# A DiT-style block of six attention layers and an FP4 feed-forward: the last layer's gate applied in its weights, FP4's margin in the scale, bias preparation moved off VectorE, stage priorities that change in time

## The chip, the cores and the metric

The kernel runs on one core of one Trainium2 chip. Times are device microseconds of one execution; a few executions are given as median with lowest and highest. The profile is of one more execution, and its span runs from the first to the last instruction of that execution.

The core's engines work side by side, each through its own queue in order: TensorE (PE: matmuls and transposes; PEld is its weight load), VectorE (DVE), ScalarE (ACT), GpSimd (POOL), and SyncE (SP), which here only issues DMAs. Results of TensorE land in PSUM, which has eight banks.

## The reference

Eight batches of 1024 tokens with 128 features, all float32. Cut to what matters:

```python
mod = (silu(c) @ wmod).reshape(8, 6, 1, 128)         # sa, ca, ga, sb, cb, gb
ga, gb = sign(ga) * max(|ga|, 0.25), likewise gb      # sign(0) = +1

h = layernorm(x) * (1 + ca) + sa
for i in range(6):                                    # 8 heads of 16
    xn = layernorm(h) * ln1_w[i] + ln1_b[i]
    q, k, v = softmax(xn @ wq[i], over 16), softmax(xn @ wk[i], over tokens), xn @ wv[i]
    h = (q @ (k.T @ v)) @ wo[i] + bo[i] + h           # per head
    xn = layernorm(h) * ln2_w[i] + ln2_b[i]
    h = leaky(xn @ w1[i]) @ w2[i] + h                 # 128 -> 512 -> 128
x = x + ga * h

h = layernorm(x) * (1 + cb) + sb
h = silu(fp4(h) @ fp4(w_gate).T) * (fp4(h) @ fp4(w_up).T)    # 128 -> 352
x = x + gb * (fp4(h) @ fp4(w_down).T)                        # 352 -> 128
```

`fp4` scales each block of 16 values by its largest magnitude over 6, rounds each to the grid 0, 0.5, 1, 1.5, 2, 3, 4, 6 (a value in the middle goes down), and scales back.

## The kernel before

A batch is one tile of 128 partitions by 1024 columns (8 chunks of 128 tokens), worked in two halves of 512 columns. Four batches are in flight at a time, each in a lane with its own buffers; batch 4 follows batch 0 in lane 0, and so on. All weights are loaded into SBUF once, within the first 50 us.

The program is not written in the order in which it runs. The function `tile_adaln_kernel` adds steps to a plan: an engine, an estimated duration, a function that issues the instructions, what it reads and writes. `Plan.order` (lines 142 to 206) then simulates the engines with these durations and picks, again and again, the step that can start earliest, and among those the one with the largest sum of its longest path to the end ("tail") and a lead. It also picks PSUM banks. It models GpSimd and some VectorE steps (`port=True`) as excluding each other. The order found is fixed for every engine's queue. Where TensorE would stand idle for longer than `GAP`, filler matmuls (`warm`, line 1250) are put in.

The leads are the table `LEAD`: for each of the eight batches eight numbers, one for each stage, where stage 0 is the first norm, 1 to 6 are the layers and 7 is the FFN. Steps added under `aside` (modulation, bias preparation) have a small negative lead of their own instead.

The parts that the change touches:

- `prepare_attn` (lines 500 to 540), once per layer: a matmul makes the 128 values that ln1's bias gives through wv; VectorE copies them out broadcast to 128x128 (line 512); a matmul with wo follows; VectorE adds bo (526) and divides by the number of heads (531); VectorE scales the rows of wv by ln1's weight (536).
- `fp4` (lines 640 to 712): largest magnitude of each block (658), over 6 with a floor (665), reciprocal (670), the reciprocal times minus one and a hair (675), the product (680), magnitude times 2^22 as bfloat16 on ScalarE (690), two VectorE steps that round by adding and subtracting a large number (694, 701), and the product with the scale on GpSimd (708). The hair, 2^-22, makes values in the middle go down.
- `prepare_ffn` (lines 715 to 766): the FP4 of the three weights, their transposes, and ScalarE's copies (749, 764).
- `layer` (from line 855): the MLP makes four hidden tiles per half (matmul 1063, ScalarE 1072), then 16 matmuls per half (1080), and VectorE adds the result onto the residual x (`onto_x`, line 1029).
- the main loop (from line 1203): after the six layers, VectorE multiplies each half of x by the gate ga (1228) and GpSimd adds the batch's input x0 (1236). Then comes `ffn`, whose `modulated_norm` takes the statistics of x (559).

Of the kernel before, what the change touches and what calls it, by code (L numbers as in the profile page):

```python
# [21 lines left out]
ROUND = 1.5 * UNIT  # L22
BANK = 512
# [59 lines left out]
class Plan:  # L83
# [7 lines left out]
    def __init__(self):  # L91
        self.steps, self.wrote, self.read, self.on = [], {}, {}, {}
        self.lead, self.batch = 0.0, -1

    def add(self, eng, occ, fn, r=(), w=(), func=None, port=False):

        s = Step()
        s.eng, s.occ, s.fn, s.func, s.lead = eng, occ, fn, func, self.lead  # L100
        s.batch, s.port = self.batch, port or eng == "POOL"
        s.lat, s.n, s.deps, s.outs = self.LAT[eng], len(self.steps), set(), []
        s.ps = list(dict.fromkeys(x for x in (*r, *w) if isinstance(x, Ps)))
        for x in s.ps:
            x.users += 1

        def keys(things):
            for x in things:
                if isinstance(x, Buf):
                    yield from x.parts  # L110
                else:
                    yield x

        r, w = list(keys(r)), list(keys(w))
        for x in (*r, *w):
            if isinstance(x, Part):
                tag = x.buf.tag
                if x.buf.after is None:
                    x.buf.after = self.on.get(tag, set())
                    self.on[tag] = set()  # L120
                s.deps |= x.buf.after
                self.on[tag].add(s.n)
        for x in (*r, *w):
            if x in self.wrote:
                s.deps.add(self.wrote[x])
        for x in w:
            s.deps.update(self.read.get(x, ()))
        for x in r:
            self.read.setdefault(x, []).append(s.n)
        for x in w:  # L130
            self.wrote[x], self.read[x] = s.n, []
        s.deps.discard(s.n)
        for x in s.ps:


            if x.first is None:
                x.first = s
            else:
                x.first.deps.update(d for d in s.deps if d < x.first.n)
        self.steps.append(s)  # L140

    def order(self, warm):
# [14 lines left out]
        table, port_free = None, 0.0  # L157
        out, todo = [], len(steps)
        while todo:
            banks = sorted(bank_free)  # L160
            best = None
            for e, c in cand.items():
                for n in c:
                    s = steps[n]
                    t = max(free[e], ready[n], port_free if s.port else 0.0)
                    need = sum(x.bank is None for x in s.ps)
                    if need:
                        t = max(t, banks[need - 1])
                    if t < INF:
                        cost = SWITCH if s.func and table and s.func != table else 0.0  # L170


                        pick = (t + cost, -s.tail - s.lead, n, t, cost)
                        if best is None or pick < best[1]:
                            best = (e, pick)
# [13 lines left out]
            end = t + cost + s.occ  # L189
# [52 lines left out]
def kernel(  # L242
# [41 lines left out]
        [1790.16, 1590.63, -133.39, -357.74, -170.79, -746.20, -949.01, -1084.50],  # L284
        [-328.73, -887.78, 125.60, 74.06, -1565.69, -372.37, -623.33, -863.15],
        [207.64, -149.66, -1586.32, -941.39, -1592.66, 94.98, -1452.11, -1239.07],
        [-746.08, 404.44, -824.95, -647.90, -118.96, -127.38, -1745.97, -425.45],
        [542.33, -1490.70, -1058.13, -1440.16, -391.61, -339.71, -149.19, -1160.38],
        [-1848.97, 2004.30, 268.43, 1104.45, -662.40, -326.99, -708.65, -1359.47],
        [573.17, -93.03, 284.47, -756.78, -278.27, -748.61, 318.91, -1786.29],  # L290
        [968.46, -558.77, 587.25, -611.65, -410.32, -941.76, -1400.05, -882.04],
    ]
    NQ = 4
# [12 lines left out]
    def stage(b, i):  # L306
        plan.lead, plan.batch = LEAD[b][i], b * len(LEAD[b]) + i

    @contextmanager
    def aside(late=40.0):  # L310

        kept = plan.lead, plan.batch
        plan.lead, plan.batch = -late, -2
        yield
        plan.lead, plan.batch = kept
# [22 lines left out]
    def load(dst, src, key, kb=64):  # L338

        if plan.batch == -1:  # L340
# [55 lines left out]
    plan.lead = 0.0  # L396
# [103 lines left out]
    def prepare_attn(l):  # L500
        t = Ps(psum)
        bv = Buf(work, [P, P], "bv", f"bv_{l}")
# [8 lines left out]
            "DVE", vec(P),  # L511
            lambda: nc.vector.tensor_copy(bv.ap(), t.ap()[:, :1].to_broadcast([P, P])),
# [5 lines left out]
                t.ap()[:, D : 2 * D], bv.ap(), wo_sb[:, l, :], start=True, stop=True  # L518
# [3 lines left out]

# [3 lines left out]
            lambda: nc.vector.tensor_tensor(mb, t.ap()[:, D : 2 * D], mb, ALU.add),  # L526
# [3 lines left out]
            "DVE", 0.14,  # L530
            lambda: nc.vector.tensor_scalar(mb, mb, 1.0 / HEADS, None, ALU.mult),
            w=[("mb", l)], port=True,
        )
        add(
            "DVE", 0.2,
            lambda: nc.vector.tensor_scalar(
                wv_sb[:, l, :], wv_sb[:, l, :], col(0, l), None, ALU.mult
            ),
            r=["cols"], w=[("wv", l)], port=True,
# [100 lines left out]
    def fp4(src, parts, ncol, n, i):  # L640

        nb = ncol // BLK
# [8 lines left out]
        def each(t):  # L651
# [13 lines left out]
            lambda: nc.vector.tensor_scalar(s(), s(), 1.0 / 6.0, 1e-12, ALU.mult, ALU.max),  # L665
# [5 lines left out]
        )  # L671

        add(
            "DVE", 0.08,
            lambda: nc.vector.tensor_scalar(r(), r(), 2.0**-22 - 1.0, None, ALU.mult),
            w=[rec], port=True,
# [18 lines left out]
                vv(), mm_(), ROUND, vv(), ALU.max, ALU.add  # L695
# [19 lines left out]
    def prepare_ffn():  # L715
# [20 lines left out]
        for n in range(2):  # L736
            t = Ps(psum)

            def turn(t=t, n=n):
# [9 lines left out]
                lambda t=t, n=n: nc.scalar.copy(wguT[:, n, :], t.ap()[:, :I]),  # L749
# [12 lines left out]
        def evict_d():  # L762
            for i, (k, kk) in enumerate(KS):
                nc.scalar.copy(wdT[:kk, i, :], u.ap()[:kk, i * D : (i + 1) * D])
# [90 lines left out]
    def layer(x, b, l, ln):  # L855
# [196 lines left out]
        _, xmT = normed(ln, x, "C", "A", l, 2, f"m{n}")  # L1052
        for h in range(H):
# [23 lines left out]
            def ymm(ty=ty, hidden=hidden):  # L1077
                for c in range(HC):
                    for j in range(NJ):
                        nc.tensor.matmul(  # L1080
                            ty.ap()[:, c * D : (c + 1) * D], hidden(j)[:, c * P : (c + 1) * P],
                            w2_sb[:, l, j, :], start=(j == 0), stop=(j == NJ - 1),
                        )

            add("PE", HC * NJ * mm(D), ymm, r=[*hT, ("w2", l)], w=[ty])
# [115 lines left out]
    for b in range(B):  # L1201
# [13 lines left out]
        for l in range(L):  # L1215
# [4 lines left out]
            layer(x, b, l, ln)  # L1220
# [3 lines left out]

        for h in range(H):
            add(
                "DVE", vec(HW),
                lambda x=x, mod=mod, h=h: nc.vector.tensor_tensor(
                    chunks(half(x, h)), chunks(half(x, h)),
                    over(mod.ap()[:, 2, :], HC), ALU.mult,  # L1230
                ),
                r=[mod[1]], w=at(x, h), port=True,
            )
            add(
                "POOL", pool2(HW) + 0.2,
                lambda x=x, b=b, h=h: nc.gpsimd.tensor_tensor(
                    half(x, h), half(x, h), half(x0s[b], h), ALU.add
                ),
                r=at(x0s[b], h), w=at(x, h),
            )  # L1240
# [18 lines left out]
    for step in plan.order(warm):  # L1259
# [50 lines left out]
```

## Time and profile before

| | |
|---|---|
| runs shown (3) | median 1429.36 us, 1426.54 to 1430.04 |
| profiled execution | 1430.2 us, its span 1428.5 us |
| TensorE clock granted | 0.999 |
| filler matmuls (line 1250) | 388 records, 49.8 us, the first at 1.6, the last at 1421.1 us |
| gate, line 1228 | 16 VectorE instructions, median 691 ns, 679 to 1466 |
| adding x0, line 1236 | 16 GpSimd instructions, median 1274 ns, 1264 to 1923 |
| matmuls of L1063 and L1080 | 350.4 and 468.3 us of TensorE's 1415.8 busy |
| stores of the result | 16 DMAs of 256 KB, 2.0 us from issue to landing |

A matmul in float32 shows as two records. Records of pipelined matmuls overlap a little, so their sum is somewhat above the time that they take in a row. The page also cuts the span into 40 equal slices, with the busy share of each engine in tenths:

```profile
PE   9999999999999999999999999999999999999998
PEld 7787877878787887877787788878887877886887
DVE  7896776667787985798978978987796775989986
ACT  5776777566677777676776867785677677777763
POOL 2020101001121220112112212111221001222232
```

TensorE is busy in every slice, but filler is among it. VectorE varies from 60% to over 90%, ScalarE is below 80% nearly everywhere, GpSimd is mostly idle. The DMA engines work in the first two slices, when the weights come in, and little afterwards.

### The profile page before, as it was taken

How to read it: one execution, taken by the hardware profiler on the slowest of the kernel's cores; microseconds unless marked ns; L12 is line 12 of the kernel's file. 1: busy time of each engine (PE TensorE's matmuls, PEld its weight loads, DVE VectorE, ACT ScalarE, POOL GpSimd, SP SyncE). 2: the span in 40 equal slices, each digit the busy share in tenths (PEclk: the TensorE clock that was granted, in tenths of full speed). 3: DMA queues.
4: the chain of work that ended last, by engine and by line, in shares of the span. 5: the costliest groups of instructions: out<-in, count | busy, mean ns of one | idle time of the engine just before them, and what ended most of it. 6: DMA issues, size and time to landing. Idle time of an engine off the chain costs nothing.

```text
span 1428.5 us, 26720 instructions
## 1 busy us (share of the span) xinstructions
PE 1415.8 (99%) x9395; PEld 1140.9 (80%) x9395; DVE 1146.0 (80%) x4560; ACT 995.9 (70%) x2280; POOL 241.8 (17%) x207
## 2 busy tenths in 40 slices
PE   9999999999999999999999999999999999999998
PEld 7787877878787887877787788878887877886887
DVE  7896776667787985798978978987796775989986
ACT  5776777566677777676776867785677677777763
POOL 2020101001121220112112212111221001222232
PEclk9999999999999999999999999999999999999999
DMA  7100000000000000000000000100000000000000
GB/s 214 47 1 1 1 1 1 1 1 1 1 22 6 16 1 1 1 27 16 1 1 28 8 1 8 27 1 8 9 1 1 1 1 1 1 16 1 16 16 15
DMA packets 16006, 18.81 MB, mean 13 GB/s; under 512 B 1552, under 2 KB 9848, under 8 KB 15872
## 3 DMA queue, kind: packets, MB, share of 16 engines
q1 hardware_dynamic: 15872, 17.10, 3.8%
q8 instruction: 74, 1.21, 0.3%
q14 instruction: 60, 0.49, 0.1%
HBM read 12.88 MB, written 4.22 MB: 12 GB/s over the span
## 4 chain that ended last, share of the span: by engine, by line
PE 82%; DVE 14%; ACT 2%; issue 1%; POOL 0%; DMA 0%; SPq 0%; DVEq 0%; POOLq 0%
PE ps L1080 23%; PE ps L1063 22%; PE ps L633 10%; PE ps L1044 5%; PE ps L977 5%; PE ps L914 5%; PE ps L867 5%; PE ps L1120 3%; PE ps L1177 2%; PE ps L1151 1%; PE warm L1250 1%; DVE x L1029 1%; DVE stats_m L559 1%; DVE nmax L874 1%; DVE qmax L923 1%; DVE stats_a L559 1%
## 5 line engine op out<-in xcount | busy, mean ns | idle before, releaser
L1063 PE MATMUL ps<-xT_m,w_sb 128*128 128x512 f32 x768 | 350.4, 595 | 1.5 <-ACT xT_m L847 1.4
L1063 PEld LDWEIGHTS ps<-xT_m,w_sb 128*128 128x128 f32 x768 | 137.5, 191 | 133.2 <-issue 91.9
L1029 DVE TENSOR_TENSOR x<-ps,x 128x512 f32<-128x512 f32 x192 | 129.5, 681 | 119.1 <-PE ps L1080 107.6
L955 POOL TENSOR_TENSOR q<-q,qsum 128x512 f32<-128x512 f32 x96 | 102.9, 1079 | 674.8 <-DVE qsum L950 374.6
L1080 PEld LDWEIGHTS ps<-w_sb,hT_D 128*128 128x128 f32 x768 | 103.9, 192 | 17.2 <-issue 13.6
L914 PEld LDWEIGHTS ps<-wq_sb,xT_a 128*128 128x128 f32 x768 | 96.6, 192 | 26.1 <-issue 16.8
L1080 PE MATMUL ps<-w_sb,hT_E 128*128 128x128 f32 x768 | 117.1, 275 | 0.0
L1080 PE MATMUL ps<-w_sb,hT_C 128*128 128x128 f32 x768 | 117.1, 275 | 0.0
L1080 PE MATMUL ps<-w_sb,hT_B 128*128 128x128 f32 x768 | 117.1, 275 | 0.0
L1080 PE MATMUL ps<-w_sb,hT_D 128*128 128x128 f32 x768 | 117.0, 275 | 0.0
L1080 PEld LDWEIGHTS ps<-w_sb,hT_B 128*128 128x128 f32 x768 | 101.4, 192 | 1.2 <-issue 0.7
L614 ACT ACTIVATE xh_a<-x,shift_a,rstd_a 128x128 f32<-128x128 f32 x192 | 83.8, 488 | 25.9 <-DVE shift_a L601 25.4
L1080 PEld LDWEIGHTS ps<-w_sb,hT_E 128*128 128x128 f32 x768 | 101.2, 192 | 0.0
L1080 PEld LDWEIGHTS ps<-w_sb,hT_C 128*128 128x128 f32 x768 | 101.2, 192 | 0.0
L914 PE MATMUL ps<-wq_sb,xT_a 128*128 128x128 f32 x768 | 99.0, 275 | 0.0
L1044 PEld LDWEIGHTS ps<-m,qT 128*128 128x128 f32 x768 | 91.1, 192 | 7.5 <-DVE m L1018 3.1
L867 PE MATMUL ps<-xT_a,wk_sb 128*128 128x512 f32 x192 | 96.7, 599 | 0.4 <-DMA wk_sb<-in_L_attn_wk_dram 0.2
L977 PEld LDWEIGHTS ps<-k,xh_a 128*128 128x128 f32 x768 | 90.7, 192 | 6.1 <-issue 4.5
L1044 PE MATMUL ps<-m,qT 128*128 128x128 f32 x768 | 95.1, 275 | 0.1
L575 ACT ACTIVATE rstd_a<-mv_a,eps 128x4 f32<-128x4 f32 x96 | 28.4, 297 | 93.9 <-DVE mv_a L561 80.4
L977 PE MATMUL ps<-k,xh_a 128*128 128x128 f32 x768 | 93.5, 275 | 0.0
L614 ACT ACTIVATE xh_m<-x,shift_m,rstd_m 128x128 f32<-128x128 f32 x192 | 81.8, 487 | 13.9 <-DVE shift_m L601 13.6
(176 smaller groups left out, 3132.5 us busy)
## 6 DMA issues: line engine op xcount, KB each, us to landing
x<-in_L_attn_x_dram SPq DMA_DIRECT2D x16, 256.0 KB, 3.2
out_dram<-x SPq DMA_DIRECT2D x16, 256.0 KB, 2.0
w_sb<-in_L_attn_w_dram SPq DMA_DIRECT2D x12, 256.0 KB, 3.9
mod<-mod_d SPq DMA_DIRECT2D x8, 256.0 KB, 4.3
mod<-mod_d SPq DMA_DIRECT2D x4, 128.0 KB, 3.3
wmod_b<-in_L_wmod_dram SPq DMA_DIRECT2D x1, 384.0 KB, 4.1
wk_sb<-in_L_attn_wk_dram SPq DMA_DIRECT2D x6, 64.0 KB, 3.0
wq_sb<-in_L_attn_wq_dram SPq DMA_DIRECT2D x6, 64.0 KB, 2.8
```

Source lines behind the costliest of these rows:

```text
L559: nc.vector.bn_stats(stats.ap()[:, c, :], s(c))
L614: nc.scalar.activation(d(c), s(c), AF.Identity, bias=shift.ap()[:, c : c + 1], scale=rstd.ap()[:, c : c + 1],)
L633: nc.tensor.transpose(t.ap()[:, c * P : (c + 1) * P], chunks(half(src, h))[:, c, :], ident)
L867: lambda tk=tk, h=h: nc.tensor.matmul(tk.ap(), wk_sb[:, l, :], half(xT, h), start=True, stop=True),
L914: nc.tensor.matmul(tq.ap()[:, c * D : (c + 1) * D], half(xT, h)[:, c * P : (c + 1) * P], wq_sb[:, l, :], start=True, stop=True,)
L955: lambda h=h, hs=hs: nc.gpsimd.tensor_tensor(heads(half(q, h)), heads(half(q, h)), each(qsum.ap()[:, hs]), ALU.mult),
L977: nc.tensor.matmul(tc_.ap()[:, :D], chunks(xh.ap())[:, c, :], chunks(k.ap())[:, c, :], start=(c == 0), stop=(c == C - 1),)
L1029: lambda: nc.vector.tensor_tensor(half(x, h), t.ap(), half(x, h), ALU.add),
L1044: nc.tensor.matmul(to.ap()[:, c * D : (c + 1) * D], half(qT, h)[:, c * P : (c + 1) * P], m.ap(), start=True, stop=True,)
L1063: lambda th=th, h=h, j=j: nc.tensor.matmul(th.ap(), w1_sb[:, l, j * P : (j + 1) * P], half(xmT, h), start=True, stop=True,),
L1080: nc.tensor.matmul(ty.ap()[:, c * D : (c + 1) * D], hidden(j)[:, c * P : (c + 1) * P], w2_sb[:, l, j, :], start=(j == 0), stop=(j == NJ - 1),)
L1120: lambda t=t, cc=cc, n=n: nc.tensor.matmul(t.ap()[:, :I], hT.ap()[:, cc * P : (cc + 1) * P], wguT[:, n, :], start=True, stop=True,),
```

## The change

Five things are done at once.

**Gate.** In the last layer, GpSimd makes a copy of the MLP's down weights with each output column multiplied by the batch's gate (`w2g`, two buffers in turn). VectorE multiplies the residual by the gate and GpSimd adds x0 once the second norm of that layer has read the residual. The MLP's matmuls then use the copy, and `onto_x` gives the gated sum with x0. The two steps after the layers are gone.

**FP4.** The step of line 675 is gone. The scale is made larger by a factor `HAIR` = 1 + 2^-22 in the constant of line 665, and the second rounding step subtracts instead of adding, as the sign is no longer turned. The results and the weights are so each larger by that factor; ScalarE's copies of the transposed weights multiply by `HAIR**-2`.

**Bias preparation.** ScalarE copies the 128 values as one column, divided by the number of heads, and the matmul reads that column broadcast. VectorE divides bo and adds the product in one step. ScalarE scales wv.

**Leads.** The numbers of `LEAD` are others. A table `TURNS` gives, for some 21 moments of the planner's clock, new leads for single stages from then on, and `Plan.order` looks a step's lead up by its stage when it picks.

**Aside.** Steps under `aside`, and those of the first preparation, have 70 subtracted from their leads (`LATE`).

```diff
+HAIR = 1.0 + 2.0**-22
...
-    def order(self, warm):
+    def order(self, leads, turns, warm):
...
         while todo:
+            while turns and turns[0][0] <= now:
+                for b, i, lead in turns.pop(0)[1]:
+                    leads[b][i] = lead
...
-                        pick = (t + cost, -s.tail - s.lead, n, t, cost)
+                        lead = leads[s.stage[0]][s.stage[1]] if s.stage else s.lead
+                        pick = (t + cost, -s.tail - lead, n, t, cost)
...
     LEAD = [
-        [1790.16, 1590.63, -133.39, -357.74, -170.79, -746.20, -949.01, -1084.50],
...
+        [2428, 4186, 594, 344, -1166, -1149, -1333, -3656],
...
+    TURNS = [
+        (75, [(1, 1, 582)]),
+        (90, [(3, 1, 625)]),
...
+        (1350, [(7, 6, -432)]),
+        (1365, [(6, 7, -1605), (7, 7, -1614)]),
+    ]
+    LATE = 70.0
...
-        plan.lead, plan.batch = -late, -2
+        plan.lead, plan.stage = -LATE - late, None
...
-        bv = Buf(work, [P, P], "bv", f"bv_{l}")
+        bv = Buf(work, [P, 1], "bv", f"bv_{l}")
...
-            "DVE", vec(P),
-            lambda: nc.vector.tensor_copy(bv.ap(), t.ap()[:, :1].to_broadcast([P, P])),
+            "ACT", 0.1, lambda: nc.scalar.mul(bv.ap(), t.ap()[:, :1], 1.0 / HEADS),
...
-                t.ap()[:, D : 2 * D], bv.ap(), wo_sb[:, l, :], start=True, stop=True
+                t.ap()[:, D : 2 * D], bv.ap().to_broadcast([P, P]), wo_sb[:, l, :],
+                start=True, stop=True,
...
-            lambda: nc.vector.tensor_tensor(mb, t.ap()[:, D : 2 * D], mb, ALU.add),
+            lambda: nc.vector.scalar_tensor_tensor(
+                mb, mb, 1.0 / HEADS, t.ap()[:, D : 2 * D], ALU.mult, ALU.add
+            ),
...
-            "DVE", 0.14,
-            lambda: nc.vector.tensor_scalar(mb, mb, 1.0 / HEADS, None, ALU.mult),
...
-            "DVE", 0.2,
-            lambda: nc.vector.tensor_scalar(
-                wv_sb[:, l, :], wv_sb[:, l, :], col(0, l), None, ALU.mult
-            ),
+            "ACT", act(D, 1) + 0.04,
+            lambda: nc.scalar.activation(
+                wv_sb[:, l, :], wv_sb[:, l, :], AF.Copy, scale=col(0, l)
+            ),
...
-            lambda: nc.vector.tensor_scalar(s(), s(), 1.0 / 6.0, 1e-12, ALU.mult, ALU.max),
+            lambda: nc.vector.tensor_scalar(s(), s(), HAIR / 6.0, 1e-12, ALU.mult, ALU.max),
...
-            lambda: nc.vector.tensor_scalar(r(), r(), 2.0**-22 - 1.0, None, ALU.mult),
...
-                vv(), mm_(), ROUND, vv(), ALU.max, ALU.add
+                vv(), mm_(), ROUND, vv(), ALU.max, ALU.subtract
...
-                lambda t=t, n=n: nc.scalar.copy(wguT[:, n, :], t.ap()[:, :I]),
+                lambda t=t, n=n: nc.scalar.mul(wguT[:, n, :], t.ap()[:, :I], HAIR**-2),
...
         _, xmT = normed(ln, x, "C", "A", l, 2, f"m{n}")
+        if l == L - 1:
+            w2g = Buf(work, [P, NJ, D], f"w2g{b % 2}", f"w2g_{b}")
+            add(
+                "POOL", pool2(NJ * D) + 0.1,
+                lambda: nc.gpsimd.tensor_tensor(
+                    w2g.ap(), w2_sb[:, l], over(mod.ap()[:, 2, :], NJ), ALU.mult
+                ),
+                r=[mod[1], ("w2", l)], w=[w2g],
+            )
+            for h in range(H):
+                add(
+                    "DVE", vec(HW),
+                    lambda h=h: nc.vector.tensor_tensor(
+                        chunks(half(x, h)), chunks(half(x, h)),
+                        over(mod.ap()[:, 2, :], HC), ALU.mult,
+                    ),
+                    r=[mod[1]], w=at(x, h), port=True,
+                )
+                add(
+                    "POOL", pool2(HW) + 0.2,
+                    lambda h=h: nc.gpsimd.tensor_tensor(
+                        half(x, h), half(x, h), half(x0s[b], h), ALU.add
+                    ),
+                    r=at(x0s[b], h), w=at(x, h),
+                )
...
-                            w2_sb[:, l, j, :], start=(j == 0), stop=(j == NJ - 1),
+                            w2g.ap()[:, j, :] if l == L - 1 else w2_sb[:, l, j, :],
+                            start=(j == 0), stop=(j == NJ - 1),
...
-        for h in range(H):
-            add(
-                "DVE", vec(HW),
-                lambda x=x, mod=mod, h=h: nc.vector.tensor_tensor(
-                    chunks(half(x, h)), chunks(half(x, h)),
-                    over(mod.ap()[:, 2, :], HC), ALU.mult,
-                ),
...
-            add(
-                "POOL", pool2(HW) + 0.2,
-                lambda x=x, b=b, h=h: nc.gpsimd.tensor_tensor(
-                    half(x, h), half(x, h), half(x0s[b], h), ALU.add
-                ),
...
```

## The prediction

> **What bounds the kernel now.** I began with the page's table of busy times, then cut the run into four stretches, once for all engines and once for the filler matmuls of line 1250 alone. Columns: stretch, length, then busy us of PE, weight loads, VectorE, ScalarE, GpSimd (first four lines); filler's PE and weight-load time (last four).
>
> ```profile
> PE 1415.8 (99%) x9395; PEld 1140.9 (80%) x9395; DVE 1146.0 (80%) x4560; ACT 995.9 (70%) x2280; POOL 241.8 (17%) x207
> 0.00:46.00 46.00, 42.84 (x288) 35.43 (x289) 38.44 (x226) 25.77 (x72) 10.00 (x18) 1.00 0.61 185
> 46.00:1340.00 1294.00, 1289.76 (x8537) 1035.30 (x8536) 1036.22 (x4163) 923.09 (x2117) 207.62 (x172) 1.00 0.02 7
> 1340.00:1384.00 44.00, 42.55 (x277) 34.33 (x277) 39.09 (x104) 29.99 (x59) 12.29 (x9) 1.00 0.02 7
> 1384.00:1428.50 44.50, 40.64 (x299) 35.81 (x297) 32.22 (x70) 17.03 (x35) 11.87 (x9) 1.00 0.07 25
> ...
> 0.00:46.00 46.00, 21.51 (x162) 20.07 (x162) 1.00 0.61 185
> 46.00:1340.00 1294.00, 4.75 (x34) 4.39 (x34) 1.00 0.02 7
> 1340.00:1384.00 44.00, 4.22 (x32) 4.10 (x33) 1.00 0.02 7
> 1384.00:1428.50 44.50, 19.28 (x162) 18.58 (x161) 1.00 0.07 25
> ```
>
> TensorE is the bound, but filler counts as busy. Time without useful matmuls is length minus busy, plus filler: 3.2 + 21.5 = 24.7 us at the start, 4.2 + 4.8 = 9.0 in the long middle, 1.4 + 4.2 = 5.7 while the last batch's MLP runs, 3.9 + 19.3 = 23.1 in its tail. Together 62.5 us; the other 1366 us are matmuls of the reference that the change neither removes nor shortens. So VectorE work saved in the middle, where TensorE is full, is worth nothing by itself; the change can only reach the 62.5 us.
>
> The chain of waits says who makes these holes: VectorE nearly without a break from 11 to 42 us, and from 1387 us the filler standing in for TensorE's wait for the last batch's FFN, whose norm and FP4 steps run on VectorE, ScalarE and GpSimd.
>
> **The gate (last layer).** Before, the result of the last MLP goes through two more steps before its statistics can start. In the timeline (start, length) of the last half to finish:
>
> ```profile
> 1381.43 0.69 DVE L1029 TENSOR_TENSOR x<-ps,x 128x512 f32<-128x512 f32 x1 [1.41 <-PE ps L1080]
> ...
> 1382.16 0.69 DVE L1228 TENSOR_TENSOR x<-x,mod 128x512 f32<-128x512 f32 x1
> ...
> 1382.98 1.28 POOL L1236 TENSOR_TENSOR x<-x,x 128x512 f32<-128x512 f32 x1 [3.96 <-DVE x L1228]
> ...
> 1384.74 0.47 DVE L559 BATCH_NORM_STATS2 stats_f<-x 128x6 f32<-128x128 f32 x2
> ```
>
> The residual is done by 1382.1, the statistics begin at 1384.7: 2.7 us. Afterwards gate and x0 are applied while the MLP's matmuls run, and the statistics follow the residual. In the middle this is hidden by other lanes; at the very end no lane is left, and it counts once: **-2.7 us**. What hides the moved steps: a half needs at least 8 x 0.43 us for L1063 and 32 x 0.112 for L1080 = 7 us from its transposed input to its residual; gate and add take 0.69 + 1.28 us and waiting, up to 1.47 + 1.92 by the longest rows. If that cover fails, the residual waits at the head of VectorE's queue, with a PSUM bank held and all later VectorE work behind it. That is the slower rival below.
>
> Added: eight GpSimd products for the scaled down weights, 128x512 with a row broadcast. Nearest row: GpSimd's L830, same shape and broadcast, 1.27 us; 10.2 us in all on an engine with over 1100 us idle. They read two constant tensors, so they can be early; one waits only for the same buffer's last use two batches before. Matmuls on the scaled weights have the same shape.
>
> A rule speaks against this. GpSimd's longest gate add took 1.92 us against a 1.27 median, and one VectorE L701 on 512 columns took 1.64 us (1391.01) against 0.69, while GpSimd ran L830: each loses up to about 1 us to the other, though the medians show no loss. The Trainium skill, "SBUF — State Buffer", section "Who interferes with whom", says that a VectorE instruction with two SBUF inputs contends with a GpSimd one that reads SBUF, and that for the shared pair the later one blocks fully. By the rule alone, eight new products block VectorE for up to 10.2 us; by the rows a collision costs 1 us and most meet none. Only collisions at the start or end, where VectorE decides, reach the sum: none to two, 0 to 2.6 us. I take 0.3, nearer the rows' medians.
>
> **FP4.** One small VectorE step per quantization goes (L675, below); the sign it carried moves into an existing step, its hair into the immediate of L665. The division by HAIR squared sits in copies that ScalarE makes anyway (L749, L764): an immediate scale, bounded by L800's 0.28 against L799's 0.26 us, five instructions, beside a full TensorE at 150 to 170 us, so nothing. In the tail one x step (1394.31 to 1394.53, 0.2 us) and one or two steps of the last quarters (0.1 to 0.3) are on the way: **-0.5 us**. The other 40-odd are hidden by full TensorE. If they did free something, 11 us of VectorE over the whole run is the upper end.
>
> **Bias preparation.** The rows, busy us and mean ns:
>
> ```profile
> L675 DVE TENSOR_SCALAR rec_g<-rec_g 128x44 f32<-128x44 f32 x32 | 7.7, 247 | 0.2
> L512 DVE COPY bv<-ps 128x128 f32<-128x128 f32 x6 | 1.6, 269 | 0.0
> L536 DVE TENSOR_SCALAR wv_sb<-wv_sb,cols 128x128 f32<-128x128 f32 x6 | 1.6, 269 | 0.0
> L526 DVE TENSOR_TENSOR mb_bc<-ps,mb_bc 128x128 f32<-128x128 f32 x6 | 1.6, 262 | 0.0
> L531 DVE TENSOR_SCALAR mb_bc<-mb_bc 128x128 f32<-128x128 f32 x6 | 1.2, 208 | 0.0
> ```
>
> Three of four VectorE steps per layer go: L512, L531, L536. L526 becomes a two-operation form; L1018, of that form at this size, takes 0.34 against 0.26. In the chain's own pieces (durations without overlap) those before 42 us are 5 of L512 at 0.2, 4 of L536 at 0.2, 4 of L531 at 0.14: 2.3 us, less 4 x 0.07 for L526 = 2.0. ScalarE gets a 128x1 copy (near L429, 0.18 us) and a 128x128 scale with one pointer, between L800 (0.28, none) and L614 (0.49, two): 0.38, six times each, 3.4 us where it is busy 25.8 of 46. Not all of the 2.0 us was in front of something late, since the preparation sits between urgent steps and moves; the DMA of the first inputs (to 5.8 us) and the first norm remain. **-1.5 us**, bounds 0 and -2.5. The broadcast stationary operand has a precedent in L791.
>
> **The order.** LEAD and LATE are new, TURNS alters leads as the planner's clock advances, and the model now holds the moved steps. An instruction's place in every queue can change, SyncE's loads and stores included. The trace holds no row for this; its bounds come from the holes. Gain at most: most of the middle's 9.0 and 5.7, and what is loose in the tail. There the first half's residual is in at 1374.8 but its FFN transposes come at 1393.9, 19 us; the rows between, added up without queueing (statistics and norm 4.1, modulation 2.0, FP4 5.0, about 0.7 waits), make some 12. So some 10 from middle and 1340 to 1384, 7 there: -17. Loss at most: as much again as today's middle, +14.7. An order with turns has more freedom than one fixed lead per stage, but it is right only on the planner's clock. Nearest row: today's middle loses 9.0 in 1294 us, so little is left there and little more is to be expected either way. I take -3.7 in the middle, about a third of the two stretches' 14.7 with 1 us of new holes set against it, and -1.7 in the tail, a quarter of the loose 7.
>
> **Sum:** -2.7 - 0.5 + 0.3 - 1.5 - 3.7 - 1.7 = -9.8 us on the profiled execution's 1430.2 us (span 1428.5 and 1.7 around it): 1420.4. The median shown is 0.8 lower; I forecast **1420 us**.
>
> **The rivals.**
> - *Same (21%).* The order gives nothing, since the middle is full and the tail is bound by FP4 on VectorE; the start's gain is eaten by the other batches' first norms. Left: -2.7 - 0.5 + 0.3: 1426.5 us. For it: VectorE is busy 39.1 of 44 us before the tail. Against: 19 us where 12 would do.
> - *Much faster (18%).* The last two batches are staggered anew, so that one's FFN fills the other's tail: holes at the end fall from 28.8 to 18, the middle loses 5, the start 2: -17.8, 1411.6. For it: 22 us of filler in the last 70. Against: both FFNs need the same VectorE, about 36 us each by its rows.
> - *Slower (12%).* The gate add comes late behind other GpSimd work or a VectorE collision, and the residual blocks VectorE's queue, then a bank, then TensorE. Place: 16 halves, all batches. It decides once the stalls that reach TensorE exceed the 9.8 us, 0.6 us a half; at 0.9 us it is +4.6: 1434. For it: GpSimd's queue stood up to 6.2 us at a wait before a gate add. Against: 7 us of cover.
> - *It does not do what it says* (in the slower share): the new order shuffles, and the middle's holes double.
>
> **Chances and range.** 49% for the forecast, own range 1416 to 1425. This kernel's runs lie within 0.25% of each other, so 0.3%, 4.3 us, is about what can be told from no change. Faster than 1425.1: nearly all of the forecast's 49, all of the 18 and a little of the same case: 0.67. Within: 0.21. Slower than 1433.6: 0.12, with the milder losses in it. The range takes in much faster and same, and most of the order's loss: 1408 to 1431.
>
> **What will show it.** The last statistics start within 0.2 us of the last MLP residual; no step between reciprocal and product in FP4; VectorE's bias steps in the first 46 us down to one per layer; filler of 46 to 1340 us below 4.8; the first half's transposes less than 17 us after its residual. Wrong if residual adds of the last layer wait for GpSimd, if filler appears in the middle, or if the tail from the last MLP matmul to the end stays 47 us long.

## The result, and the profile after

The changed kernel takes **1419.09 us** (median of 4 runs, 1418.72 to 1420.03) against 1429.66 us: a ratio of 0.9932, 95% interval 0.9915 to 0.9949. The forecast was 1420 us. The profiled execution took 1418.9 us, with a span of 1417.3.

The page's line of busy times, then the run in four stretches cut at the last MLP matmul (1374.43 us; 1381.41 before), for all engines and then for the filler of line 1289 alone; the columns are those of the prediction's first fence:

```profile
PE 1400.6 (99%) x9257; PEld 1124.6 (79%) x9257; DVE 1148.7 (81%) x4491; ACT 987.7 (70%) x2286; POOL 249.7 (18%) x215
...
0.00:46.00 46.00, 42.34 (x278) 34.62 (x278) 39.00 (x225) 31.86 (x92) 11.31 (x19) 1.00 0.62 188
46.00:1340.00 1294.00, 1286.75 (x8478) 1029.13 (x8477) 1049.65 (x4118) 914.61 (x2112) 215.05 (x182) 1.00 0.02 6
1340.00:1374.43 34.43, 32.87 (x227) 27.08 (x226) 29.44 (x83) 22.73 (x46) 11.80 (x9) 1.00 0.05 16
1374.43:1417.30 42.87, 38.67 (x280) 33.72 (x278) 30.57 (x67) 18.55 (x39) 11.53 (x8) 0.98 0.08 32
...
0.00:46.00 46.00, 17.35 (x124) 15.91 (x124) 1.00 0.62 188
46.00:1340.00 1294.00, 4.47 (x30) 3.81 (x30) 1.00 0.02 6
1340.00:1374.43 34.43, 0.00 (x0) 0.00 (x0) 1.00 0.05 16
1374.43:1417.30 42.87, 11.70 (x96) 11.27 (x96) 0.98 0.08 32
```

The last two stretches of the kernel before, cut at its own last MLP matmul, for all engines and then for its filler, and the same two of e12, the last of the experiments below:

```profile
1340.00:1381.41 41.41, 39.97 (x253) 31.74 (x253) 37.30 (x99) 28.28 (x54) 11.27 (x8) 1.00 0.02 7
1381.41:1428.50 47.09, 43.23 (x322) 38.40 (x321) 34.01 (x74) 18.74 (x39) 12.89 (x9) 1.00 0.06 23
...
1340.00:1381.41 41.41, 4.10 (x30) 3.87 (x30) 1.00 0.02 7
1381.41:1428.50 47.09, 19.39 (x162) 18.80 (x162) 1.00 0.06 23
```

```profile
1340.00:1374.46 34.46, 32.90 (x228) 27.06 (x227) 30.47 (x81) 22.90 (x47) 10.21 (x9) 1.00 0.05 17
1374.46:1417.50 43.04, 38.94 (x285) 33.99 (x283) 30.92 (x67) 17.35 (x36) 11.55 (x8) 1.00 0.08 31
...
1374.46:1417.50 43.04, 13.26 (x110) 12.83 (x110) 1.00 0.08 31
```

Length less busy time plus filler gives the time without useful matmuls ("holes"). Beside it stand two kernels of the experiments, cut in the same way at their own last MLP matmul:

| holes, us | before | after | old parts, own order (e10) | all parts, other order (e12) |
|---|---|---|---|---|
| 0 to 46 | 24.7 | 21.0 | 22.7 | 22.7 |
| 46 to 1340 | 9.0 | 11.7 | 9.3 | 8.2 |
| 1340 to the last MLP matmul | 5.5 | 1.6 | 0.0 | 1.6 |
| from there to the end | 23.3 | 15.9 | 20.7 | 17.4 |
| last MLP matmul ends at | 1381.4 | 1374.4 | 1371.3 | 1374.5 |
| length of the tail | 47.1 | 42.9 | 45.9 | 43.0 |

All four execute the same 9007 useful matmuls (instructions less filler), yet their busy times less filler lie between 1364.5 and 1367.7 us. Matmul ends are modelled, so hole sums of two kernels compare to about 3 us; spans and starts are not affected by that.

Before to after, the holes fall at the start (3.7), in front of the last MLP matmul (4.0) and in the tail (7.4), and rise by 2.7 in the long middle. VectorE's busy time did not fall, though 69 of its instructions are gone.

The signs named in the prediction, in the timeline of VectorE (start, length):

```profile
1374.52 0.69 DVE L1054 TENSOR_TENSOR x<-ps,x 128x512 f32<-128x512 f32 x1 [0.33 <-PE ps L1132]
1375.25 0.87 DVE L587 BATCH_NORM_STATS2 stats_f<-x 128x6 f32<-128x128 f32 x4
```

The last statistics follow the last residual without a gap. Before, 3.3 us lay between the two starts, now 0.7. No residual of line 1054 waited for the gate's add on GpSimd. The view puts one wait of the last layer (1.26 us before 1367.67) down to GpSimd's FP4 product, but TensorE's last matmul for that residual also ends only 0.1 us before it. In the groups of the first 46 us, the bias steps are one on VectorE and two on ScalarE (the sixth of L557 comes at 70.6 us):

```profile
L557 DVE SCALAR_TENSOR_TENSOR mb_bc<-mb_bc,ps 128x128 f32<-128x128 f32 x5 | 1.3, 270 | 0.0
...
L564 ACT ACTIVATE wv_sb<-wv_sb,cols 128x128 f32<-128x128 f32 x6 | 2.4, 399 | 0.0
L543 ACT ACTIVATE bv<-ps 128x1 f32<-128x1 f32 x6 | 1.0, 168 | 0.1
```

In the FP4 groups no VectorE row is left between the reciprocal (L701) and the product (L705). The first half's transposes come 14.4 us after its residual (19.1 before). The chain of waits has one long piece of filler near its end (start, length):

```profile
1403.88 4.91 PE warm L1289 x44
```

Of the chain's two long filler pieces, 6.03 and 5.14 us, only the second is left. All of the tail's gain lies ahead of the last batch's first FFN matmul, before and after:

```profile
1395.24 5.00 PE L1120 MATMUL ps<-wguT,hTf 128*128 128x352 f32 x16
...
1384.03 5.00 PE L1176 MATMUL ps<-wguT,hTf 128*128 128x352 f32 x16
```

From the last MLP matmul to this one it took 13.8 us and takes 9.6; from here to the end it is 33.3 us in both.

So the total came as forecast. What the signs cannot tell is which part of the change, if any, made it.

### The profile page after: what moved, and what is told of

It is laid out like the page before. It is cut to its first block, busy times and chain, and to the rows that moved or that the text cites. A ratio compares the mean times of both kernels' runs of the same rounds, so it can differ in the third digit from the quotient of the medians.

```text
span 1417.3 us, 26401 instructions
## 1 busy us (share of the span) xinstructions
PE 1400.6 (99%) x9257; PEld 1124.6 (79%) x9257; DVE 1148.7 (81%) x4491; ACT 987.7 (70%) x2286; POOL 249.7 (18%) x215
## 5 line engine op out<-in xcount | busy, mean ns | idle before, releaser
L1132 PEld LDWEIGHTS ps<-w_sb,hT_D 128*128 128x128 f32 x640 | 86.8, 192 | 15.0 <-issue 11.7
L1132 PE MATMUL ps<-w_sb,hT_E 128*128 128x128 f32 x640 | 97.6, 275 | 0.0
L1132 PE MATMUL ps<-w_sb,hT_C 128*128 128x128 f32 x640 | 97.6, 275 | 0.0
L1132 PE MATMUL ps<-w_sb,hT_B 128*128 128x128 f32 x640 | 97.6, 275 | 0.0
L1132 PE MATMUL ps<-w_sb,hT_D 128*128 128x128 f32 x640 | 97.5, 275 | 0.0
L872 ACT ACTIVATE xT_a<-ps,cols 128x512 f32<-128x512 f32 x96 | 72.1, 775 | 19.2 <-PE ps L661 18.8
L587 DVE BATCH_NORM_STATS2 stats_a<-x 128x6 f32<-128x128 f32 x384 | 82.9, 278 | 2.9 <-POOL x L855 0.9
L1132 PEld LDWEIGHTS ps<-w_sb,hT_B 128*128 128x128 f32 x640 | 84.4, 192 | 0.5 <-ACT xh_m L642 0.2
```

The costliest lines, as they stand in the source:

```text
L587: nc.vector.bn_stats(stats.ap()[:, c, :], s(c))
L872: lambda t=t, h=h: nc.scalar.activation(half(xT, h), t.ap(), AF.Identity, bias=col(params + 1, l), scale=col(params, l),),
L1132: nc.tensor.matmul(ty.ap()[:, c * D : (c + 1) * D], hidden(j)[:, c * P : (c + 1) * P], w2g.ap()[:, j, :] if l == L - 1 else w2_sb[:, l, j, :],
```

## The experiments

The kernel before, run on the same chips, took 1429.06 us beside the first four experiments, 1429.22 beside the next four and 1429.03 beside the last four. Medians and ratios are to these. My theory at the start was the prediction's: parts and order each bring about half, and add up.

**Parts alone, in the order of before (e1 to e4).** The planner's sequence of the kernel before was written out as a fixed list, filler included. Then single parts were put into it: the gate and x0 steps right behind the second reader of the residual, the scaled weights at the norm's statistics.

```diff
-            w2_sb[:, l, j, :]
+            w2g.ap()[:, j, :] if l == L - 1 else w2_sb[:, l, j, :]
...
+            hooks[("w2g", f"m{n}", 0)] = [1, scaled]
+            hooks[("gate", f"m{n}", h)] = [2, lambda h=h: gated(h)]
```

> The gate alone in the kernel before, with the order of before kept in every queue: the gate and x0 steps move to just behind the last read of the residual by the last layer's second norm, the scaled weights are made at that norm's statistics, all else stays in its place. Theory A (the prediction: the two steps count once, in the tail): 2.7 us less than before, 1426 to 1427.5, the last statistics within 0.2 us of the last MLP residual, the tail from the last MLP matmul to the end 44.4 instead of 47.1 us, middle unchanged. Theory B (a fixed order hides it: the steps behind the statistics stand in line behind other work anyway, so the gain needs a new order): less than 1 us, tail above 46 us. Theory C (collisions on the shared port or late adds): slower than before by 1 us or more.

Measured: **1441.99 us**, ratio 1.009 (1.0077 to 1.0103). The last MLP matmul ends at 1393.2 us, 11.8 later: none of this in the tail. VectorE's timeline near it shows one way in which that comes about:

```profile
1372.42 0.69 DVE L877 TENSOR_TENSOR x<-x,mod 128x512 f32<-128x512 f32 x1 [0.45 <-ACT xh_m L624]
1373.03 1.54 DVE L616 TENSOR_SCALAR xh_m<-x,mv_m,rstd_m 128x128 f32<-128x128 f32 x2
```

The gate step (L877) overwrites the residual, so it has to wait for ScalarE's last read of it. It stands at the head of VectorE's queue meanwhile, and the other half's normalization, which TensorE needs, comes behind it. Twelve of the sixteen gate steps find VectorE idle so, 6.3 us in all. TensorE's largest wait of that kernel is for just this row:

```profile
PE ps L644 <- DVE xh_m L616: 2.9, 4, 0.9
```

> FP4's step with the hair taken out alone, order of before kept. Theory A: 0.5 us less, 1429, all of it in the tail. Theory B: nothing that can be told (within 0.3 us), since the step's place in the queue is followed by a wait in the tail too. Theory D (VectorE decides in the middle as well): 2 us or more less, the middle's holes below 9.0 us.

```diff
-            lambda: nc.vector.tensor_scalar(s(), s(), 1.0 / 6.0, 1e-12, ALU.mult, ALU.max),
+            lambda: nc.vector.tensor_scalar(s(), s(), HAIR / 6.0, 1e-12, ALU.mult, ALU.max),
...
-            lambda: nc.vector.tensor_scalar(r(), r(), 2.0**-22 - 1.0, None, ALU.mult),
+            lambda: None,
```

Measured: 1427.58 us, ratio 0.9989 (0.9983 to 0.9996), so 0.6 to 2.4 us, with a tail of 46.7 us (47.1 before).

> The bias preparation alone, order of before kept, each of its steps at its old place but on ScalarE where the change puts it. Theory A: 1.5 us less, 1428, holes of the first 46 us at 23.2 instead of 24.7. Theory B: less than 0.5 us, because the first inputs and norms decide. Theory E (VectorE alone decides from 11 to 42 us): 2 to 2.5 us less.

```diff
-            lambda: nc.vector.tensor_copy(bv.ap(), t.ap()[:, :1].to_broadcast([P, P])),
+            lambda: nc.scalar.mul(bv.ap(), t.ap()[:, :1], 1.0 / HEADS),
...
-            lambda: nc.vector.tensor_scalar(wv_sb[:, l, :], wv_sb[:, l, :], col(0, l), None, ALU.mult),
+            lambda: nc.scalar.activation(wv_sb[:, l, :], wv_sb[:, l, :], AF.Copy, scale=col(0, l)),
```

Measured: 1428.88 us, ratio 0.9998 (0.999 to 1.0006). The first MLP matmul starts 0.4 us earlier (44.69 for 45.10), but in e5, which keeps the old bias steps, it starts at 44.61, so this is not the edit's. The end does not move.

> Gate, FP4 and bias together, order of before kept. Theory A: their sum, 4.4 us less, 1425, so that about 6 of the change's 10.6 us are the order's. Theory B: 1 to 2 us less, 9 are the order's. Theory F (the parts do it, the leads only follow): 8 us or more less.

All three edits together: 1442.5 us, ratio 1.0091 (1.0076 to 1.0106), against all three theories. In the order of before the parts cost 13 us.

**The gate placed with care (e5).** One objection is that the hand-placed hooks of e1 were clumsy. So the sequence of before was kept for all other steps, the planner put each moved step where its inputs were ready and its engine was free before the next old step, and filler was spaced anew.

```diff
+            ahead = [
+                k for k in loose
+                if n < 0 or left[n] or (steps[k].eng == steps[n].eng and start(k) <= start(n))
+            ]
+            if ahead:
+                n = min(ahead, key=start)
```

> The gate alone again, the rest in the order of before, but each moved step is put into its queue only where its inputs are due before the next step in line could start, and the filler is spaced anew. Theory G (the first run's 13 us are its placement: a gate step stood at the head of VectorE's queue, waiting for ScalarE's half of the norm, and the old filler stayed): no slower than before, 1426 to 1429. Theory H (the old order has no room for them at these places: VectorE is full when a last layer's MLP runs, and whatever is put in front there delays a norm): still 4 us or more slower than before, holes between 46 us and the last MLP at 14 or more instead of 14.6 in all of before's 46 to 1384, tail within 1 us of 47.

Measured: 1441.15 us, ratio 1.0085 (1.007 to 1.0101). That is e1's within the intervals: neither placement finds these steps a free place in the old sequence. The gate steps' wait for ScalarE is down to 1.6 us (3 of them), and TensorE waits about as little as before, but it gets 61.2 us of filler instead of 49.8. So the wait at the head of VectorE's queue alone does not make the 12 to 13 us. What the planned filler stands in for I did not trace.

**Parts taken back out of the new order (e6, e7).** In e6 the last four batches alone get their gate and x0 back behind the residual, with plain down weights. In e7 VectorE does the four bias steps again, in the places of the new ones.

```diff
+        late = l == L - 1 and b + LANES >= B
...
-                lambda: nc.gpsimd.tensor_tensor(
+                lambda: None if late else nc.gpsimd.tensor_tensor(
...
-            onto_x(ty, h)
+            onto_x(ty, h, late)
```

> The changed kernel with its own order, but in the last four batches the gate and x0 steps stand behind the last residual again, on unscaled weights, everything else at its place. Theory A: 2.7 us more than the changed kernel, 1421.8, all of it behind the last MLP matmul (45.6 instead of 42.9 us), because there the two steps count once. Theory I (the order of the changed kernel leans on the moved steps in the middle too): 6 us or more. Theory B: less than 1 us.

Measured: 1431.18 us, ratio to before 1.0017 (1.001 to 1.0024), so 12 us above the changed kernel. In the profile the last MLP matmul ends 6.3 us later and the tail is 5.4 us longer (48.3); the granted clock of 0.57 between 1392 and 1396 us makes about 1.7 of these 5.4 (4 us times 0.43). TensorE is busy 2 us less between 570 and 1140 us, long before any tail. Over the run its waits for VectorE's half of the second norm (3.0 us for 1.3) and for ScalarE's kT (2.9 us for 0.4) have grown.

```diff
-            lambda: nc.scalar.mul(bv.ap(), t.ap()[:, :1], 1.0 / HEADS),
+            lambda: nc.vector.tensor_copy(bv.ap(), t.ap()[:, :1].to_broadcast([P, P])),
...
+                nc.vector.tensor_scalar(mb, mb, 1.0 / HEADS, None, ALU.mult),
```

> The changed kernel with its own order, the bias preparation on VectorE again, at the same places. Theory A: 1.5 us more, 1420.6, in the first 46 us. Theory E: 2 to 3.7 us more, since these steps account for the whole gain at the start (24.7 to 21.0 us without useful matmuls). Theory B (new leads make the gain there): less than 0.5 us.

Measured: 1424.21 us, ratio 0.9965 (0.9952 to 0.9978), 5.1 us above the changed kernel and above all three theories. The first MLP matmul starts at 52.06 instead of 45.50. TensorE's waits, then its stretches (busy, granted clock, DMA share, GB/s) in this kernel:

```profile
PE ps L548 <- DVE bv L543: 3.2, 4, 1.4
```

```profile
30.00:36.00 6.00, 4.93 (x38) 1.00 0.73 225
36.00:40.00 4.00, 2.99 (x15) 0.70 0.21 61
40.00:44.00 4.00, 4.00 (x19) 0.50 0.00 0
```

and the same stretches of the changed kernel:

```profile
30.00:36.00 6.00, 5.57 (x46) 1.00 0.62 183
36.00:40.00 4.00, 3.57 (x26) 1.00 0.13 43
40.00:44.00 4.00, 4.00 (x31) 1.00 0.01 2
```

The waits for VectorE's copy add up to 3.2 us. Then the granted clock falls to a half: 16 matmuls of line 1070 take 3.76 us there, the same 16 took 2.02 in the changed kernel (line 1069). This profiled execution is the slowest of the five, 1426.05 us with a mean granted clock of 0.997. The fastest, 1423.25 us, has 1.000, which leaves no room for such a fall, and is still 4.2 us above the changed kernel. So the fall is part of the cost in some executions only. The rest fits the waits, 3.2 us where I had put the bounds at 0 and 2.5; no profile without the fall was taken, so that is not shown.

At this point one could have concluded that the parts carry the gain: taking one out costs 5 or 12 us. But an order made for some steps can be disturbed by any other steps, whichever way round. The next runs separate the two.

**The new leads without the new parts, and the reverse (e8, e9).** In e8 the steps of before are planned with the new leads, turns and LATE; in e9 the new steps with the old leads:

```diff
-        [2428, 4186, 594, 344, -1166, -1149, -1333, -3656],
+        [1790.16, 1590.63, -133.39, -357.74, -170.79, -746.20, -949.01, -1084.50],
...
+    TURNS = []
+    LATE = 0.0
```

> The steps of before, planned with the new leads, turns and LATE. Theory A (leads and turns bring 5.4 us by themselves, the parts the rest): 1423 to 1425. Theory J (leads only fit the steps that they were made for, and unfit ones cost more than the parts bring): 1432 or more.

Measured: 1511.61 us, ratio 1.0579 (1.0563 to 1.0595).

> All parts of the change, planned with the leads of the kernel before and none of the turns. Theory K (leads fit only the steps for which they were found, as the 1511.6 of the old parts under the new leads suggests): slower than before, 1440 to 1480, with the holes all over the middle. Theory L (the parts carry the gain and the new leads only add to it): 1420 to 1428.

Measured: 1455.19 us, ratio 1.0182 (1.0165 to 1.0199), with 23.6 us of holes between 46 and 1340. Leads fit only the steps they were found for. "What the new leads are worth for the old parts" has no answer until old parts get leads of their own.

**Each set of parts with its own order (e10 to e12).** For three sets of steps I searched leads and turns anew, starting from the leads of before: small random changes, kept as a rule where the planner's own plan then ended earlier. Only the two tables differ from the changed kernel, and in e10 and e11 the parts that are put back. The searches were of the same kind, one for each set; how much a second search would move a time was not measured.

```diff
-        [2428, 4186, 594, 344, -1166, -1149, -1333, -3656],
+        [6025, 2274, 3409, -1326, 1404, 2236, 947, -1826],
...
```

> The steps of before (late gate by VectorE, four FP4 steps, four VectorE bias steps) under the new planner, with leads and turns searched anew for these steps, from the leads of before. Theory S (the gain is the new order; the parts could stay as they were): 1417 to 1421, as the changed kernel. Theory P (the order gives about half and the parts, by what they allow, the other half): 1423 to 1427, 2 to 6 under before, and the tail behind the last MLP matmul stays above 46 us, since the late gate chain is still in it. Theory N (the order of before was as good as these steps allow): 1428 to 1431.

Measured: **1420.11 us** (1418.93 to 1420.44, 4 runs), ratio 0.9937 (0.9922 to 0.9952). Theory S held; my own theory P, which gave half to the parts, fell. With the late gate, the FP4 step of L675 and four VectorE bias steps, a new order alone reaches the changed kernel within the intervals. Its stretches, then its filler:

```profile
0.00:46.00 46.00, 43.17 (x298) 36.46 (x299) 38.28 (x211) 28.21 (x76) 11.55 (x19) 1.00 0.60 187
46.00:1340.00 1294.00, 1287.75 (x8510) 1031.86 (x8509) 1050.47 (x4195) 917.27 (x2117) 206.94 (x174) 1.00 0.02 7
1340.00:1371.31 31.31, 31.27 (x208) 25.32 (x206) 27.08 (x82) 19.98 (x43) 6.82 (x5) 1.00 0.05 17
1371.31:1417.20 45.89, 41.83 (x308) 36.89 (x306) 32.69 (x74) 18.53 (x39) 13.14 (x9) 1.00 0.07 24
...
0.00:46.00 46.00, 19.83 (x152) 18.71 (x152) 1.00 0.60 187
46.00:1340.00 1294.00, 3.03 (x22) 2.69 (x22) 1.00 0.02 7
1340.00:1371.31 31.31, 0.00 (x0) 0.00 (x0) 1.00 0.05 17
1371.31:1417.20 45.89, 16.65 (x136) 16.05 (x136) 1.00 0.07 24
```

Up to the last MLP matmul TensorE has next to no hole from 1340 us on, and that matmul ends 3.1 us before the changed kernel's. The late gate is still there, in VectorE's timeline:

```profile
1371.32 0.69 DVE L1077 TENSOR_TENSOR x<-ps,x 128x512 f32<-128x512 f32 x1 [0.36 <-PE ps L1128]
1372.04 0.69 DVE L1276 TENSOR_TENSOR x<-x,mod 128x512 f32<-128x512 f32 x1
...
1374.58 0.87 DVE L607 BATCH_NORM_STATS2 stats_f<-x 128x6 f32<-128x128 f32 x4 [0.16 <-POOL x L1284]
```

From residual to statistics it takes 3.3 us where the changed kernel takes 0.7, and the tail is 3.0 us longer. Earlier end of the MLP and longer tail cancel.

> The gate in the down weights with x0 added meanwhile, bias preparation and FP4 steps of before, leads and turns searched anew for these steps. Theory P1 (the gate carries the gain by its shorter tail, 2.7 us and more): 1419 to 1422. Theory P2 (the gate pays only where the VectorE work of the bias and FP4 steps is gone as well): 1423 to 1427, with the tail at 43 us, 3 to 4 under before, and the time given back as holes ahead of the last MLP matmul.

Measured: 1426.77 us (20 runs), ratio 0.9984 (0.9978 to 0.9991). The tail is 44.2 us, but 14.2 us of holes stand between 46 and 1340, and the last MLP matmul ends at 1381.4, as in the kernel before. P2's time held; the tail is 1.2 us longer than it said and the gain, 2.3 us, smaller. I do not take it as shown that the gate needs the other parts: a search that ends worse may just have found less. Then one search may miss by several us, as this one lies 6.7 us above e10.

> The changed kernel's steps with leads and turns found by the same search from the leads of before, so another order than the changed kernel's. Theory P: within 1.5 us of the changed kernel, 1418 to 1421, tail about 43 us: the steps, not one lucky order, set the time. Theory M (the changed kernel's order is a rare find): 1423 or more.

Measured: **1419.05 us** (1417.85 to 1419.23), ratio 0.9929 (0.9914 to 0.9944). A different order with the same steps gives the same time: 1419.09 is no lucky find. No version was found that beats the changed kernel by more than can be measured.

Put together, in us:

| steps | order of before | leads of before | leads of the change | own search |
|---|---|---|---|---|
| those of before | 1429.0 (1429.7 beside the result) | the same kernel | 1511.6 | 1420.1 |
| gate alone | 1442.0 and 1441.2 | not run | not run | 1426.8 |
| all of the change | 1442.5 | 1455.2 | 1419.1 | 1419.05 |

The change's 10 us: about **9 are had by order alone**. For the three parts 1.0 us is left between e10 and either kernel with all parts, which these intervals cannot tell from nothing. That the old steps can reach 1420.1 is shown; what the parts are worth beyond is only as sure as single searches are.

A rival is the clock. In its profile the kernel before has one stretch of half clock in mid-run, which costs about 1.7 us (see the last section), and e10 has none. Over the 82 executions of the kernel before, the 30 with a mean granted clock of 1.000 have a median of 1428.7 us, the 45 with 0.999 one of 1429.5. So the clock makes about 1 us of the 9 at most.

## Why the prediction was right, and where it was not

The time, 1420 for 1419.09, was right; the sum it came from was divided wrongly, so that it came right was luck.

- **What bounds the kernel**: right. The gain came from holes, up to about 1 us of it from the clock, and none from VectorE's work in the middle.
- **The gate, -2.7**: the size was right where it was read (its two rows give 2.6, not 2.7): 2.6 us less from residual to statistics, 2.9 to 3.0 us less tail where both sets of steps have an order of their own. What failed is "it counts once" as a saving of the whole. With late gate the last MLP matmul can end 3.1 us earlier, so the span does not shrink by it. Why the moved steps hold it up by 3 us I could not settle; e1 shows one way in which they can, the wait on the residual's readers at the head of VectorE's queue, and e5 that it is not the only one.
- **"What hides the moved steps"**: I compared 7 us of cover with the steps' own durations and with waits for GpSimd. The wait that came in e1 was another, for ScalarE's read of the residual. A slower kernel came in the old order (12 to 13 us, above the rival's 4.6), though not by the rival's cause; in the new order, planned with these steps, it did not come.
- **Port collisions, +0.3**: right. The eight new products took 1266 to 1507 ns, median 1290, near the row they were priced by; the sixteen gate steps took 653 to 693 ns. One product held VectorE, as the prediction's rule has it: a step with two SBUF inputs, issued just behind it, took 1.21 us for a median of 0.16 and ended with it.

```profile
724.11 1.27 POOL L1084 TENSOR_TENSOR w2g<-w_sb,mod 128x512 f32<-128x512 f32 x1 [1.96 <-PE ps L1132]
...
724.18 1.21 DVE L629 SCALAR_TENSOR_TENSOR shift_a<-mv_a,rstd_a 128x4 f32<-128x4 f32 x1
```

During the other seven no VectorE step was stretched, so of the rule's 10.2 us about 1.1 came, in mid-run.

- **FP4, -0.5**: alone -1.5 us (0.6 to 2.4), of the sign predicted. The tail, where I had put all of it, is 0.4 us shorter; where the rest falls was not isolated.
- **Bias, -1.5**: alone -0.2 us, inside the bounds. Returned to the new order it cost 5.1, outside them: the profile shows 3.2 us of waits and a fall of the clock, and an execution without such a fall still costs 4.2. The start's holes fell by 3.7 us, but e10 has 2.0 of these with the old bias steps, and e12 has 22.7 with the new ones as e10 has without.
- **The order, -5.4**: this is the term that failed. Its worth with the old parts is **-9.0 us** (1429.03 to 1420.11; the interval gives 6.9 to 11.1). "Little is left in the middle" was right: from 46 to 1340 the holes are 9.0 before, 9.3 in e10, 8.2 in e12 and 11.7 after. The room was elsewhere. In e10 the holes fall by 2.0 us at the start, where I gave the order nothing, by 5.5 from 1340 us to the last MLP matmul, and by 2.5 in the tail. So the term that was too small is the -3.7 for what stands ahead of the last MLP matmul: there 7.2 us of holes went. The tail is 1.2 us shorter by order alone, near the -1.7.
- **Adding parts and order**: the order -3.6 too small and the parts -4.4 counted beside it made up for each other. With an order of its own for each set, the parts came to 1.0 us and not 4.4.
- **The rivals' times**: "same" (1426.5) and "much faster" (1411.6) were both missed by 7 us. The holes from 1340 on fell from 28.8 to 17.5, as "much faster" had it, but the middle and the start together gave 1 us, not 7.
- **The signs**: all came true, though the middle's holes rose by 2.7 us while its filler fell. In e10, the time came without most of them: the statistics come 3.3 us after the residual, the old bias and FP4 steps are all there. They proved that the edits did locally what was planned, not that the edits paid.

## What to carry to other kernels

Where a static order has been tuned to its steps, a part tried in the old order can look much worse than it is (the gate, 12 to 13 us slower), and a part taken out of the new order can look worth more than it is (5 and 12 us); only the old steps with an order searched as hard as the new one's say what the part is worth. A chain shortened at the very end is a gain only if what stands ahead of it still ends when it did. So search the order first, and change the steps after it.

## What was not expected of the hardware

**The clock fell on short waits, and not every time.** In e7 the longest single wait of TensorE near 37 us was 1.41 us, and between 30 and 36 us it was busy 4.93 of 6 us, yet the granted clock fell to 0.50 between 40 and 44 us. The Trainium skill, "TensorE: Matmul & The Clock Gate", Part 1 (the clock gate), has the half rate return after an idle window of about 3.4 us; here several short gaps were enough. By the rule these gaps would cost just their 3.2 us, by the measurement the first MLP matmul came 6.6 us later, with the slowed matmuls among it. Nor does the gap alone decide. The kernel before (first two lines, then its granted clock) and e10 (last two) have the same single gap of 2.28 us and then the same four matmuls:

```profile
647.23 0.66 PE L633 MATMUL ps<-ident,xh_a 128*128 128x128 f32 x4 [2.28 <-ACT g L1128]
647.73 3.09 PE L1063 MATMUL ps<-xT_m,w_sb 128*128 128x512 f32 x4
649.00:650.00 1.00, 1.00 (x3) 0.50 0.06 16
...
643.82 0.66 PE L681 MATMUL ps<-ident,xh_a 128*128 128x128 f32 x4 [2.28 <-ACT g L1176]
644.31 1.88 PE L1111 MATMUL ps<-xT_m,w_sb 128*128 128x512 f32 x4
```

In the kernel before the clock fell behind it (0.57 from 648 to 652 us, so about 1.7 us of time, 4 us times 0.43), in e10 it stayed at 1.00.

**The first matmuls are slow in some executions and not in others.** In the profile of e2 the two 512-column matmuls at the start took 594 ns each, in that of the kernel before 1038 (with a granted clock of 1.00 shown in both), and the first MLP matmul started 2.4 us earlier (42.68 for 45.10) with nothing changed ahead of it but small FP4 steps. Single executions of this kernel differ by such an amount: its times lie in two groups, around 1426.5 and 1429.2 us. That the start makes the two groups is not shown.

**VectorE's busy time moved without any change of its work.** The page of e12 has:

```profile
PE 1399.9 (99%) x9261; PEld 1123.3 (79%) x9261; DVE 1137.2 (80%) x4491; ACT 988.4 (70%) x2290; POOL 250.3 (18%) x215
```

The changed kernel has the same 4491 VectorE instructions at 1148.7 us, 11.5 us more, and ends within 0.1 us of it. The instructions did not get slower: count times mean, added up over all VectorE rows, gives 1457 us in both. Records of neighbouring instructions overlap, as the statistics at 1375.25 us end at 1376.12 and the next step starts at 1376.04, and busy time counts the overlap once. So the 11.5 us are a difference in overlap. A busy sum of an engine that is not the bound tells little of what its work costs.
